# A graph layer's kernel: row decoding by two matmuls, an absolute value and a saturating addition, with 48 groups picked whole

## The chip, the cores and the metric

The kernel runs on one core of one Trainium2 chip. The metric is device microseconds of one execution, the median over several runs. Engines are named as in the profile: PE (TensorE matmuls), PEld (its weight loads), DVE (VectorE), ACT (ScalarE), POOL (GpSimd) and SP (SyncE, which issues most DMAs).

## The reference, cut to what matters

A graph layer over 6250 nodes of 64 features and 206250 edges, sorted by target node.

```python
h = jnp.maximum(_layernorm(x, axis=-1), 0.0)          # the table of node rows
msg = jax.nn.relu(h[src] + edge_attr)                 # one row per edge
agg = jax.ops.segment_sum(msg, dst, num_segments=6250)
z = h + agg
x = x + (jax.nn.relu(z @ W1 + b1) @ W2 + b2)
```

All of it is float32. The costly parts are `h[src]`, a gather of 206250 rows of 256 bytes from a table that the kernel itself makes, and the segment sum.

## The kernel before, in words

**Groups, sets, units.** Edges come in groups of 768 (128 partitions, 6 columns each), 269 groups in all. The first five are handled in the head. The others are bound into sets (`GROUPS`, line 63): a set is two groups, or one. Each set has six columns of 128 edges whose rows are *picked* by PE. In a set of two groups these are the last three columns of each group, and the other three columns of each (six in all) are *gathered* by POOL with one indirect DMA per column (`gather`, line 236). In a set of one group all six columns are picked and POOL gathers nothing for it; such a group is listed in `WHOLE`. Before the change there are 150 sets, 36 of them of one group. The loop (`both_units`, line 942) runs one unit per set; units alternate between even and odd ones, which have their work written out in two different orders. The order on each engine is the order in which the code stands, nothing is rescheduled.

**Picking.** The table stands in SBUF as two float16 parts per value (`hp`: 64 columns of high parts, 64 of low parts). DVE compares (`find` line 594, tile `found`; `back` line 606, tile `backs`) make one-hot matrices in float16; PE multiplies with them (`across_of` line 624, tile `half`), ACT copies the result to SBUF (`across`), PE transposes (`turn`), ACT copies again (`picked`), PE picks (`pick`, line 652). ACT copies the picked rows to the float16 tile `both` (`decode_parts`, line 716).

**Decoding.** The high part carries, as its sign, one more bit for the last place of the value. `decode_minus` (line 722) lets DVE make `minus`, the negated negative part of `both`. `decode_sum` (line 727) adds up, for each of six 128-column pieces, three matmuls of 64 columns in the PSUM bank `joint`: `both` with `join` (high times 2048 plus low), `minus` with `weigh_sign` (which turns the sign of the high part round), `minus` with `weigh_last` (the last place). `decode_add` (line 739) adds the result, scaled, from `joint` to the edge rows `ea` on DVE; `xg_add` (line 747) adds the gathered rows on DVE; `messages` (line 753) is one relu over the set's `ea` on ACT, a unit after the addition; `window_sum` (line 769) sums the messages on PE by one-hot matmuls of float32. The decoded sums and the window sums share the bank `joint`, in different columns. `sums` run only in even units, for two sets at a time.

**Queues.** SP issues the loads of `sources` and `spots` (768 KB each, once in two units), of the edge rows (`attr_set`, line 258) and the stores. POOL issues the gathers. Those of the first `AHEAD` = 6 sets are issued before the loop; the others stand in `pending` (line 269), and `passes` (line 273) issues one of them each time that the PE work written so far, added up from planned nanoseconds, has grown by `SPREAD` (1110 ns in the first 18 units, 1190 ns behind). A gather so issued carries a dependency on the PE instruction at which it was issued, so it cannot start before that instruction is done. The rows go into a ring of `RING` = 10 tiles `xg`. `ranked` and `counted_by_columns` prepare, once in three units, where each edge's row is to be found (`rank_of` and its neighbours).

Of the kernel before, what the change touches and what calls it, by code (L numbers as in the profile page):

```python
# [9 lines left out]

F32 = mybir.dt.float32
# [9 lines left out]
P = 128  # L21
G = 6
# [19 lines left out]
H = 3  # L42
# [16 lines left out]
HEAD, PAIR = 2 * RG - 1, 4 * RG - 3  # L59
SINGLES, DOUBLES = 3, 11  # L60
assert F0 + SINGLES * HEAD + DOUBLES * PAIR == NG + 1 and SETS == 3
# [16 lines left out]
PLACED = [0, 2, 6, 22, 38, NCH]  # L78
RING, AHEAD, EAS = 10, 6, 4
SPREAD = 1110, 1190  # L80
# [8 lines left out]
def kernel(  # L89
# [25 lines left out]
    FIRST = (F0 + HEAD) * G  # L115
# [61 lines left out]
    weigh_sign = const.tile([P, D], F16, name="weigh_sign")  # L177
    weigh_last = const.tile([P, D], F16, name="weigh_last")
    nc.vector.scalar_tensor_tensor(join, ident[:, :D], FINE, ident[:, D:], op0=ALU.mult, op1=ALU.add)
    for t, by in ((weigh_sign, 2 * FINE), (weigh_last, -FINE * HALF_LAST)):  # L180
        nc.vector.tensor_scalar_mul(t, ident[:, :D], by)
# [122 lines left out]
    def stretches(t_sb, c0, c1):  # L304

        wide = c0 >= 2 * SINGLES
        n, size, chunks = ((c1 - c0) // 4, PAIR, 4) if wide else ((c1 - c0) // 2, HEAD, 2)
# [173 lines left out]
    def ln_rows(r, n, v):  # L481
        h = x_rows(r, n)
        nc.vector.reciprocal(v, v)
        nc.vector.tensor_scalar_mul(v, v, UP)
# [18 lines left out]
    def ln_turned():  # L503
        zv = z[:D, :NP].rearrange("d (p r) -> d p r", r=RR)
        for pt, r, n in turned_rows:
            nc.scalar.activation(zv[:, :, r:r + n], pt[:, :n].rearrange("d u p -> d p u"), AF.Copy, scale=1.0 / UP)
        turned_rows.clear()

    def ln_parts(r, m, h):
# [3 lines left out]
        nc.scalar.copy(hi, h)  # L513
        nc.scalar.mul(rest, h, FINE)
# [9 lines left out]
        nc.vector.tensor_tensor(hi, hi, sign, ALU.mult)  # L524

    def add_attr(y, xg, ea):
        nc.vector.scalar_tensor_tensor(y, xg, 1.0 / UP, ea, op0=ALU.mult, op1=ALU.add)

    def combine(xg, ea, n):
        add_attr(xg[:, :n], xg[:, :n], ea[:, :n])  # L530
        nc.scalar.activation(ea[:, :n], xg[:, :n], AF.Relu)
        return ea
# [171 lines left out]
    def first_messages(g):  # L704
        ea, xg = ring(eas, g), rows_of(g)
        if g < RAW:
            yield from norm_edges(xg)
            nc.vector.tensor_tensor(ea, ea, xg, ALU.add)
        else:
            add_attr(ea, xg, ea)  # L710
        nc.scalar.activation(ea, ea, AF.Relu)
        msgs[g] = ea
# [25 lines left out]
    def decode_add(k):  # L738
        n = len(GROUPS[k])
        ea = eas[(k + RAWS) % EAS][:, :n]  # L740
        to = ea[:, :, G - H:] if n == 2 else ea[:, 0].rearrange("p (i j) d -> p i j d", i=2)
        to = to.rearrange("p i j d -> p i (j d)")
        nc.vector.scalar_tensor_tensor(to, joint[:, :2 * H * D].rearrange("p (i s) -> p i s", i=2),  # L743
                                       1.0 / (UP * FINE), to, op0=ALU.mult, op1=ALU.add)

    def xg_add(k):
        if len(GROUPS[k]) == 2:
            ea, xg = eas[(k + RAWS) % EAS], xgs[(k + RAWS) % RING]
            to = ea[:, :, :G - H].rearrange("p g j d -> p g (j d)")
            nc.vector.scalar_tensor_tensor(to, xg.rearrange("p g j d -> p g (j d)"), 1.0 / UP, to, op0=ALU.mult, op1=ALU.add)  # L750
# [180 lines left out]
    def joint_out(k):  # L931
        decode_add(k)
# [7 lines left out]
    def both_units(k):  # L940
# [7 lines left out]
        if odd:  # L948
# [20 lines left out]
            if k > 1:  # L969
                messages(k - 2)  # L970
# [11 lines left out]
            next(decoding, None)  # L982
            weave(compared, counted, others)
# [8 lines left out]
        else:  # L992
# [5 lines left out]
            if k > 1:  # L998
                messages(k - 2)
# [32 lines left out]
            next(decoding, None)  # L1032
# [279 lines left out]
```

## Time and profile before

| | before |
|---|---|
| median of three runs | 992.82 us (987.42 to 995.36) |
| the profiled execution | 989.2 us, its span 987.4 us |
| busy, share of the span: PE | 905.7 us, 92% |
| DVE | 922.7 us, 93% |
| ACT | 780.2 us, 79% |
| POOL | 749.1 us, 76% |
| mean granted PE clock | 0.968 |

The span runs from the first to the last instruction of the program on the core; 1.8 us of the profiled execution lie outside it. Busy time counts an instant once however many instructions of an engine overlap in it. [...] For ACT and DVE the profile's duration of an instruction also overlaps a little with its successor.

### The profile page before, as it was taken

What the parts mean: (1) busy time and instruction counts of PE and PEld (TensorE: products, weight loads), DVE (VectorE), ACT (ScalarE), POOL (GpSimd) and SP (SyncE); (2) the same over time, 40 slices, a digit from 0 to 9 for tenths busy, and PEclk for the clock granted to TensorE, in tenths of its full rate; (3) what the DMA queues carried; (4) which work ended last, traced back from release to release, by engine and by line L of the source; (5) the groups of instructions that cost most, each with busy time, mean ns of one, the idle gap of its engine ahead of it and who ended that gap; (6) DMA issues with size and microseconds to landing.
All of it is one profiled execution on the core that took longest, in us unless ns stands there. A gap on an engine that the chain in (4) does not pass through costs nothing.

```text
span 987.4 us, 35954 instructions
## 1 busy us (share of the span) xinstructions
PE 905.7 (92%) x13996; PEld 728.2 (74%) x13996; DVE 922.7 (93%) x2314; ACT 780.2 (79%) x1623; POOL 749.1 (76%) x727
## 2 busy tenths in 40 slices
PE   2249999999999989999999999999999999999986
PEld 1137777878877778787887777887877787787874
DVE  8898999989999999999999899999999999999975
ACT  6528888878888878888888788887887888888873
POOL 7877777777777777777777777777777777777771
PEclk9559999999999999999999999999999999999998
DMA  7436667666766666776766766766766666676841
GB/s 222 140 100 196 192 230 232 208 226 210 217 218 210 216 216 205 223 240 217 225 215 205 227 215 212 261 202 202 243 214 212 223 217 228 214 234 208 272 146 36
DMA packets 93833, 205.63 MB, mean 208 GB/s; under 512 B 24537, under 2 KB 62042, under 8 KB 93658
## 3 DMA queue, kind: packets, MB, share of 16 engines
q1 hardware_dynamic: 70762, 179.87, 51.1%
q0 software_dynamic: 22784, 23.38, 12.8%
q8 instruction: 112, 1.84, 0.7%
q14 instruction: 63, 0.52, 0.2%
q10 hardware_dynamic: 112, 0.03, 0.0%
HBM read 199.07 MB, written 4.13 MB: 206 GB/s over the span
## 4 chain that ended last, share of the span: by engine, by line
PE 60%; DVE 19%; DMA 12%; issue 3%; ACT 3%; DVEq 1%; POOL 1%; SPq 0%; ACTq 0%; POOLq 0%
PE pick L655 19%; PE half L633 13%; DMA xg<-h_rows,src_sb 9%; PE joint L769 8%; PE turn L644 7%; DVE backs L611 6%; PE joint L734 6%; DMA sources<-source_row 2%; PE rows L432 2%; DVE ea L743 2%; DVE found L601 2%; ACT ea L755 2%; PE rows L366 1%; PE half L628 1%; PE rows L808 1%
## 5 line engine op out<-in xcount | busy, mean ns | idle before, releaser
L241 POOL DMA_INDIRECT xg<-h_rows,src_sb x682 | 711.5, 1043 | 207.9 <-issue 52.7
L655 PE MATMUL pick<-backs,picked 128*128 128x384 f16 x1800 | 437.4, 328 | 0.0
L650 ACT COPY picked<-turn 128x512 f16<-128x512 f16 x450 | 262.6, 584 | 69.2 <-PE turn L644 62.0
L639 ACT CAST across<-half 128x512 f16<-128x512 f32 x450 | 264.9, 589 | 18.6 <-PE half L633 10.5
L633 PE MATMUL half<-found,hp 128*128 128x128 f16 x3600 | 276.5, 220 | 0.0
L611 DVE TENSOR_SCALAR backs<-spots,ids 128x1536 f16<-128x1536 int16 x450 | 275.4, 647 | 0.0
L633 PEld LDWEIGHTS <-hp 128*128 128x128 f16 x3600 | 234.5, 98 | 37.9 <-issue 0.6
L601 DVE TENSOR_SCALAR found<-sources,nodes_of 128x1536 f16<-128x1536 int16 x300 | 191.8, 672 | 1.1 <-issue 0.8
L655 PEld LDWEIGHTS <-picked 128*128 128x128 f16 x1800 | 157.3, 99 | 34.0 <-issue 0.3
L644 PE MATMUL turn<-ident_h,across 128*128 128x128 f16 x1800 | 175.8, 220 | 1.7 <-ACT picked L650 1.7
L755 ACT ACTIVATE ea<-ea 128x768 f32<-128x768 f32 x150 | 115.6, 770 | 55.0 <-DVE ea L743 50.5
L644 PEld LDWEIGHTS <-across 128*128 128x128 f16 x1800 | 123.0, 98 | 38.8 <-issue 6.0
L720 ACT CAST both<-pick 128x384 f16<-128x384 f32 x300 | 146.0, 487 | 3.2 <-PE pick L655 3.2
L769 PEld LDWEIGHTS joint<-oh,ea 128*64 128x64 f32 x3176 | 101.2, 138 | 48.9 <-DVE ea L743 24.6
L769 PE MATMUL joint<-oh,ea 128*64 128x32 f32 x3176 | 112.5, 224 | 20.3 <-DVE ea L743 11.6
L734 PE MATMUL joint<-join,both 128*128 128x64 f16 x900 | 127.0, 194 | 0.0
L734 PE MATMUL joint<-weigh_sign,minus 128*128 128x64 f16 x900 | 126.5, 194 | 0.6 <-DVE minus L724 0.5
L734 PE MATMUL joint<-weigh_last,minus 128*128 128x64 f16 x900 | 126.4, 194 | 0.0
L734 PEld LDWEIGHTS <-minus 128*128 128x128 f16 x1800 | 96.9, 98 | 16.5 <-DVE minus L724 1.3
L743 DVE SCALAR_TENSOR_TENSOR ea<-joint,ea 128x384 f32<-128x384 f32 x150 | 82.0, 547 | 22.5 <-PE joint L734 21.7
L734 PEld LDWEIGHTS <-both 128*128 128x128 f16 x900 | 88.1, 99 | 1.7
L696 DVE TENSOR_TENSOR oh<-slot,slots 128x384 f32<-128x384 int16 (+1 forms) x151 | 76.1, 504 | 0.1
(131 smaller groups left out, 777.0 us busy)
## 6 DMA issues: line engine op xcount, KB each, us to landing
sources<-source_row SPq DMA_DIRECT2D x75, 768.0 KB
spots<-spot_rows SPq DMA_DIRECT2D x75, 768.0 KB
ea<-in_edge_attr_dram SPq DMA_DIRECT2D x112, 384.0 KB
xg<-h_rows,src_sb POOLq DMA_INDIRECT x682
ea<-in_edge_attr_dram SPq DMA_DIRECT2D x44, 192.0 KB
xb<-in_x_dram SPq DMA_DIRECT2D x12, 128.0 KB
out_dram<-o SPq DMA_DIRECT2D x12, 128.0 KB
h_rows<-x SPq DMA_DIRECT2D x3, 384.0 KB
```

What stands on the lines that cost most here:

```text
L241: it = nc.gpsimd.indirect_dma_start(out=xg[:, j, :], out_offset=None, in_=rows[:, :], in_offset=bass.IndirectOffsetOnAxis(ap=idx[:, j:j + ...
L601: nc.vector.tensor_scalar(found[d][:, b * PARTS + m:b * PARTS + m + PARTS // 2].rearrange("p m u s -> p (m u s)"), sources[d][:, m * 4 * S ...
L611: nc.vector.tensor_scalar(backs[2 * d + u // 2][:, q].rearrange("p u v e -> p (u v e)"), spots[d].bitcast(I16)[:, u * VERSIONS * H * P:(u ...
L633: last = nc.tensor.matmul(ps[:, j * P:(j + 1) * P], hp[:, b * PARTS + m].rearrange("p t d -> p (t d)"), found[d][:, b * PARTS + m].rearran ...
L639: nc.scalar.copy(across[d, q].rearrange("p u j s -> p j u s"), ps.rearrange("p (j u s) -> p j u s", j=J, u=4))
L644: passes(nc.tensor.transpose(ps[:, u * P:(u + 1) * P], ac[:, u].rearrange("p j s -> p (j s)"), ident_h), 56)
L650: nc.scalar.copy(picked[d][:, q].rearrange("p u d -> p (u d)"), turned.pop((d, q)))
L655: it = nc.tensor.matmul(pick_banks[(2 * k + i) % 3][:, :H * P], picked[d][:, q, u], backs[k][:, q // VERSIONS, i, q % VERSIONS, :], start= ...
L720: nc.scalar.copy(fetched[k][:, i], pick_banks[(2 * k + i) % 3][:, :H * P])
L734: it = nc.tensor.matmul(to, rows[:, i, j * P:(j + 1) * P], weights, start=(n == 0), stop=(n == len(terms) - 1))
L755: nc.scalar.activation(msg, msg, AF.Relu)
L769: last = nc.tensor.matmul(pa[i * D:(i + 1) * D], msg[:, j, :], oh[:, j, :], start=(j < lo + 2), stop=(j >= G - 2))
```

## The change

The sign of the picked high part is no longer turned round by a matmul: both parts of the table now carry the sign (`ln_parts` multiplies high and low part by it), so the joined sum comes out negated or not, `weigh_last` takes the sign that fits, and an absolute value on ACT (`decode_out`) makes the row and scales it, out of PSUM into a new float32 tile `exact` of two buffers. `minus` is made by ACT. The additions on DVE become a custom instruction, `TENSOR_ADD_SAT`, which adds two tensors and limits the sum, here from below by 0: addition and relu in one. So `messages` is no longer an ACT instruction, and its place in the units falls away. The table of rows is no longer scaled by 4096 in memory. And the sets are cut otherwise: 156 sets, of which 48 have one group; four sets' gathers instead of six stand ahead of the loop. In the built programs 646 gathers of `h_rows` into `xg` stand in place of 682; 30 of the 682 stood ahead of the loop, and 18 of the 646 do.

```diff
-HEAD, PAIR = 2 * RG - 1, 4 * RG - 3
-SINGLES, DOUBLES = 3, 11
+ONE, TWO = 2 * RG - 1, 2 * RG - 2
+SINGLES, DOUBLES = 4, 22
...
-for h in range(SINGLES + 2 * DOUBLES):
-    last = h >= SINGLES and (h - SINGLES) % 2
+for h in range(SINGLES + DOUBLES):
     GROUPS += [(g, g + 1), (g + 2,), (g + 3, g + 4)]
     g += 5
-    GROUPS += [(g, g + 1), (g + 2,), (g + 3, g + 4)] if last else [(g, g + 1), (g + 2, g + 3), (g + 4, g + 5)]
-    g += 5 if last else 6
+    GROUPS += [(g, g + 1), (g + 2,), (g + 3, g + 4)] if h >= SINGLES else [(g, g + 1), (g + 2, g + 3), (g + 4, g + 5)]
+    g += 5 if h >= SINGLES else 6
...
-RING, AHEAD, EAS = 10, 6, 4
-SPREAD = 1110, 1190
+RING, AHEAD, EAS = 10, 4, 4
+SPREAD = 1112, 1267
...
-        nc.vector.tensor_tensor(hi, hi, sign, ALU.mult)
-
-    def add_attr(y, xg, ea):
-        nc.vector.scalar_tensor_tensor(y, xg, 1.0 / UP, ea, op0=ALU.mult, op1=ALU.add)
+        both = hp[:, r:r + m]
+        nc.vector.tensor_tensor(both, both, sign.unsqueeze(2).to_broadcast([PP, m, 2, D]), ALU.mult)
+
+    def add_relu(ea, xg):
+        nc.vector._custom_dve(TENSOR_ADD_SAT, out=ea, in0=xg, in1=ea, s0=float("inf"), s1=0.0)
...
-        nc.vector.tensor_scalar(minus, fetched[k], -1.0, 0.0, op0=ALU.mult, op1=ALU.max)
+        nc.scalar.activation(minus, fetched[k], AF.Relu, scale=-1.0)
...
-                terms = (both, join), (minus, weigh_sign), (minus, weigh_last)
+                terms = (both, join), (minus, weigh_last)
...
-    def decode_add(k):
-        n = len(GROUPS[k])
-        ea = eas[(k + RAWS) % EAS][:, :n]
-        to = ea[:, :, G - H:] if n == 2 else ea[:, 0].rearrange("p (i j) d -> p i j d", i=2)
-        to = to.rearrange("p i j d -> p i (j d)")
-        nc.vector.scalar_tensor_tensor(to, joint[:, :2 * H * D].rearrange("p (i s) -> p i s", i=2),
-                                       1.0 / (UP * FINE), to, op0=ALU.mult, op1=ALU.add)
+    exact = {}
+
+    def decode_out(k):
+        exact[k] = work.tile([P, 2, H * D], F32, name="exact", bufs=2)
+        nc.scalar.activation(exact[k].rearrange("p i s -> p (i s)"), joint[:, :2 * H * D], AF.Abs, scale=1.0 / (UP * FINE))
...
-        nc.scalar.activation(msg, msg, AF.Relu)
+        to = msg[:, :, G - H:] if len(gs) == 2 else msg[:, 0].rearrange("p (i j) d -> p i j d", i=2)
+        add_relu(to.rearrange("p i j d -> p i (j d)"), exact.pop(k))
...
     def joint_out(k):
-        decode_add(k)
+        messages(k)
...
-            if k > 1:
-                messages(k - 2)
...
             next(decoding, None)
             next(decoding, None)
+            decode_out(k - 1)
             weave(compared, counted, others)
```

On ACT, in one unit in the middle of the loop before the change, the relu of an earlier set (`ea`) stands among the copies:

```order
L650 COPY picked<-turn 128x512
L639 CAST across<-half_194 128x4x4x32
L720 CAST both<-pick_198 128x384
L755 ACTIVATE ea_150<-ea_150 128x768
L650 COPY picked<-turn 128x512
L639 CAST across<-half_195 128x4x4x32
L720 CAST both<-pick_199 128x384
L650 COPY picked<-turn 128x512
L639 CAST across<-half_194 128x4x4x32
```

In the changed kernel a unit at a like place reads so; `exact` is the absolute value out of PSUM, and `minus` the negated part:

```order
L735 ACTIVATE exact<-joint 128x384
L636 CAST across<-half_192 128x4x4x32
L713 CAST both<-pick_195 128x384
L717 ACTIVATE minus<-both 128x768
L647 COPY picked<-turn 128x512
L636 CAST across<-half_193 128x4x4x32
L713 CAST both<-pick_196 128x384
L647 COPY picked<-turn 128x512
L636 CAST across<-half_192 128x4x4x32
L647 COPY picked<-turn 128x512
L735 ACTIVATE exact<-joint 128x384
```

So ACT has two instructions per set, one of 768 and one of 384 elements, where it had one of 768 (384 in a set of one group).

On DVE, the end of an even unit and the start of the odd one behind it, before:

```order
L743 SCALAR_TENSOR_TENSOR ea_147<-joint,ea_147 128x2x192
L687 ISA
L687 TENSOR_TENSOR z<-z,joint 128x32
...
L696 TENSOR_TENSOR oh<-slot,slots 128x384
L750 SCALAR_TENSOR_TENSOR ea_148<-xg_152,ea_148 128x2x192
L724 TENSOR_SCALAR minus<-both 128x768
L611 TENSOR_SCALAR backs<-spots,ids 128x1536 x3
```

And in the changed kernel, where the rows named ISA at L525 are the custom instruction:

```order
L525 ISA ea_145<-exact,ea_145 128x2x192
L684 ISA
L684 TENSOR_TENSOR z<-z,joint 128x32
...
L693 TENSOR_TENSOR oh<-slot,slots 128x384
L608 TENSOR_SCALAR backs<-spots,ids 128x1536
```

`minus` has left DVE, and the addition at the end of a unit reads `exact`, which ACT writes, in place of `joint`, which PE writes.

## Rows read from the trace of the kernel before

**Rows 1.** Busy time by stretch: PE, PEld, DVE, ACT, POOL, clock, DMA; the loop
```profile
100.00:950.00 850.00, 832.39 (x13096) 672.33 (x13094) 814.21 (x2023) 703.96 (x1482) 657.85 (x631) 1.00 0.68 220
```

**Rows 2.** One line's instructions: the picks, 12 per set; min/median/max ns, first to last
```profile
L655 PE MATMUL pick<-backs,picked x1800: 323/326/524, 79.7 to 973.1; 128*128 128x384 f16 x180
```

**Rows 3.** Groups of instructions on DVE: busy us, mean ns; idle before
```profile
L611 DVE TENSOR_SCALAR backs<-spots,ids 128x1536 f16<-128x1536 int16 x450 | 275.4, 647 | 0.0
L601 DVE TENSOR_SCALAR found<-sources,nodes_of 128x1536 f16<-128x1536 int16 x300 | 191.8, 672 | 1.1 <-issue 0.8
L743 DVE SCALAR_TENSOR_TENSOR ea<-joint,ea 128x384 f32<-128x384 f32 x150 | 82.0, 547 | 22.5 <-PE joint L734 21.7 <-PE turn L644 0.7
L750 DVE SCALAR_TENSOR_TENSOR ea<-xg,ea 128x384 f32<-128x384 f32 x114 | 62.7, 550 | 0.5 <-issue 0.5
L724 DVE TENSOR_SCALAR minus<-both 128x768 f16<-128x768 f16 x150 | 54.1, 361 | 2.9 <-ACT both L720 2.9
L375 DVE TENSOR_REDUCE rank_of<-rows 128x18 f16<-128x432 f32 x50 | 29.9, 597 | 0.8 <-PE rows L366 0.8
...
L379 DVE SCALAR_TENSOR_TENSOR spot<-part,rank_of 128x18 int16<-128x18 f16 x50 | 9.0, 179 | 0.1
...
L524 DVE TENSOR_TENSOR hp<-hp,sign 128x768 f16<-128x768 f16 x3 | 1.7, 552 | 1.3 <-ACT sign L522 1.3
```

**Rows 4.** Timeline of DVE: start us, duration us; the negated part and its successor
```profile
562.91 0.35 DVE L724 TENSOR_SCALAR minus<-both 128x768 f16<-128x768 f16 x1
563.18 0.59 DVE L375 TENSOR_REDUCE rank_of<-rows 128x18 f16<-128x432 f32 x1
```

**Rows 5.** Who waited for whom: us in total, times, longest us
```profile
ACT ea L755 <- DVE ea L743: 50.5, 52, 3.2
PEld joint L769 <- DVE ea L743: 24.6, 35, 2.6
DVE ea L743 <- PE joint L734: 21.7, 27, 5.3
DVE found L596 <- DMA sources<-source_row: 13.2, 18, 3.1
PEld joint L769 <- ACT ea L755: 9.8, 19, 1.8
```

**Rows 6.** Groups of instructions on ACT
```profile
L720 ACT CAST both<-pick 128x384 f16<-128x384 f32 x300 | 146.0, 487 | 3.2 <-PE pick L655 3.2
L755 ACT ACTIVATE ea<-ea 128x768 f32<-128x768 f32 x114 | 96.5, 847 | 52.0 <-DVE ea L743 48.0 <-DVE backs L611 3.8
L755 ACT ACTIVATE ea<-ea 128x384 f32<-128x384 f32 x36 | 19.0, 528 | 3.0 <-DVE ea L743 2.5 <-issue 0.2
L522 ACT ACTIVATE sign<-sign 128x768 f16<-128x768 f16 x3 | 2.4, 828 | 0.0
```

**Rows 7.** Timeline of ACT: a relu of 768 elements and the copy behind it
```profile
609.37 0.84 ACT L755 ACTIVATE ea<-ea 128x768 f32<-128x768 f32 x1 [1.38 <-DVE ea L743]
610.12 0.57 ACT L650 COPY picked<-turn 128x512 f16<-128x512 f16 x1
```

**Rows 8.** Group of the gathers on POOL
```profile
L241 POOL DMA_INDIRECT xg<-h_rows,src_sb x682 | 711.5, 1043 | 207.9 <-issue 52.7 <-PE pick L655 36.0 <-PE half L633 27.4
```

**Rows 9.** Busy time by stretch, tile `xg` alone: additions on DVE, gathers on POOL
```profile
87.00:966.00 879.00, 61.02 (x111) 680.51 (x652) 0.99 0.68 218
```

**Rows 10.** The chain that ended last: start us, us, what
```profile
552.54 0.17 PE joint L734 x6
552.71 0.22 PE turn L644 x4
...
553.11 0.33 PE pick L655 x2
553.43 0.45 PE half L633 x8
...
554.38 5.43 DMA xg<-h_rows,src_sb
```

More of the change, by code (lines that the diff above doesn't have):

```diff
@@ L9 @@
 from concourse._compat import with_exitstack
+from concourse.dve_ops import TENSOR_ADD_SAT
 F32 = mybir.dt.float32
@@ L58 @@
 RG = 2 * SETS
-HEAD, PAIR = 2 * RG - 1, 4 * RG - 3
-SINGLES, DOUBLES = 3, 11
-assert F0 + SINGLES * HEAD + DOUBLES * PAIR == NG + 1 and SETS == 3
+ONE, TWO = 2 * RG - 1, 2 * RG - 2
+SINGLES, DOUBLES = 4, 22
+assert F0 + SINGLES * ONE + DOUBLES * TWO == NG + 1 and SETS == 3
 GROUPS = []
 g = F0
-for h in range(SINGLES + 2 * DOUBLES):
-    last = h >= SINGLES and (h - SINGLES) % 2
+for h in range(SINGLES + DOUBLES):
     GROUPS += [(g, g + 1), (g + 2,), (g + 3, g + 4)]
     g += 5
-    GROUPS += [(g, g + 1), (g + 2,), (g + 3, g + 4)] if last else [(g, g + 1), (g + 2, g + 3), (g + 4, g + 5)]
-    g += 5 if last else 6
+    GROUPS += [(g, g + 1), (g + 2,), (g + 3, g + 4)] if h >= SINGLES else [(g, g + 1), (g + 2, g + 3), (g + 4, g + 5)]
+    g += 5 if h >= SINGLES else 6
 KS = len(GROUPS)
@@ L77 @@
 QW = Q // VERSIONS
-PLACED = [0, 2, 6, 22, 38, NCH]
-RING, AHEAD, EAS = 10, 6, 4
-SPREAD = 1110, 1190
+PLACED = [0, 2, 8, 24, 40, NCH]
+RING, AHEAD, EAS = 10, 4, 4
+SPREAD = 1112, 1267
 UP, FINE = 2.0 ** 12, 2.0 ** 11
@@ L114 @@
     dst_sb = const.tile([P, CP], I32, name="dst_sb")
-    FIRST = (F0 + HEAD) * G
+    FIRST = (F0 + ONE) * G
     nc.sync.dma_start(out=src_sb[:, :FIRST], in_=src_main[:, :FIRST])
@@ L176 @@
     join = const.tile([P, D], F16, name="join")
-    weigh_sign = const.tile([P, D], F16, name="weigh_sign")
     weigh_last = const.tile([P, D], F16, name="weigh_last")
     nc.vector.scalar_tensor_tensor(join, ident[:, :D], FINE, ident[:, D:], op0=ALU.mult, op1=ALU.add)
-    for t, by in ((weigh_sign, 2 * FINE), (weigh_last, -FINE * HALF_LAST)):
-        nc.vector.tensor_scalar_mul(t, ident[:, :D], by)
+    nc.vector.tensor_scalar_mul(weigh_last, ident[:, :D], FINE * HALF_LAST)
     upper = const.tile([P, P], F16, name="upper")
@@ L306, in stretches @@
         wide = c0 >= 2 * SINGLES
-        n, size, chunks = ((c1 - c0) // 4, PAIR, 4) if wide else ((c1 - c0) // 2, HEAD, 2)
+        n, size, chunks = (c1 - c0) // 2, TWO if wide else ONE, 2
         assert n * chunks == c1 - c0 and (wide or c1 <= 2 * SINGLES)
@@ L505, in ln_turned @@
         for pt, r, n in turned_rows:
-            nc.scalar.activation(zv[:, :, r:r + n], pt[:, :n].rearrange("d u p -> d p u"), AF.Copy, scale=1.0 / UP)
+            nc.scalar.copy(zv[:, :, r:r + n], pt[:, :n].rearrange("d u p -> d p u"))
         turned_rows.clear()
@@ L512, in ln_parts @@
         sign = lnp.tile([PP, m, D], F16, name="sign")
-        nc.scalar.copy(hi, h)
-        nc.scalar.mul(rest, h, FINE)
+        nc.scalar.mul(hi, h, UP)
+        nc.scalar.mul(rest, h, UP * FINE)
         yield
@@ L707, in first_messages @@
             yield from norm_edges(xg)
[L708 to L712, printed above, removed]
+        msgs[g] = combine(xg, ea, G)
         yield
@@ L748, in xg_add @@
             ea, xg = eas[(k + RAWS) % EAS], xgs[(k + RAWS) % RING]
-            to = ea[:, :, :G - H].rearrange("p g j d -> p g (j d)")
-            nc.vector.scalar_tensor_tensor(to, xg.rearrange("p g j d -> p g (j d)"), 1.0 / UP, to, op0=ALU.mult, op1=ALU.add)
+            add_relu(ea[:, :, :G - H].rearrange("p g j d -> p g (j d)"), xg.rearrange("p g j d -> p g (j d)"))
     def messages(k):
@@ L997, in both_units @@
                 decode_minus(k - 1)
-            if k > 1:
-                messages(k - 2)
             next(picking, None)
@@ L1032, in both_units @@
             next(decoding, None)
+            if k:
+                decode_out(k - 1)
             next(picking, None)
@@ L1208 @@
     decode_minus(KS - 1)
-    messages(KS - 2)
     for k in (KS - 2, KS - 1):
@@ L1213 @@
     weave(joined(KS - 1))
+    decode_out(KS - 1)
     xg_add(KS - 1)
     weave(joint_out(KS - 1))
-    messages(KS - 1)
     weave(sums(KS - 1))
```

4 lines of the change are left out of this document (1 added, 3 removed).

## The prediction

> **What bounds the kernel now.** I read the page's busy shares first, then the loop alone by stretches. Between 100 and 950 us DVE is busy 814.2 of 850 us, 95.8%, ACT 82.8%, POOL 77%, PE 97.9% [rows 1]. PE's share is no load: a pick lasts 326 ns [rows 2], but in the chain two follow each other in 0.33 us, eight half matmuls take 0.45, four turns 0.22, six decode matmuls 0.17 [rows 10]. The picks, 12 per set, run from 79.7 to 973.1 us [rows 2]: 893 us for 150 sets, T = 5.96 us per set. Of this DVE works 0.958 x 5.96 = 5.71 us and ACT 4.94.
>
> The waits say who bounds whom. DVE's own waits are few: 21.7 us for PE's decode sums in 27 sets and 13.2 us for the `sources` load [rows 5]. PE and ACT wait for DVE: ACT's relu 50.5 us, PE's window sums 24.6 us, and 9.8 us more for that relu [rows 5]. So DVE sets the pace, with a chain DVE addition, ACT relu, PE window sums, PE decode, DVE addition that closes on it.
>
> The engine that its share hides is POOL. From 87 to 966 us it does 652 gathers [rows 9], 1.348 us each. Its idle time is 207.9 us over 682 gathers, 0.30 each [rows 8]: the same short gap before every one, no long wait at all. So POOL is working back to back through the whole loop, behind the pace that the code plans for it, and its last gathers come within ten microseconds of the last pick. DVE's additions of gathered rows nevertheless idle only 0.5 us [rows 3], so the gathers are in time, by the lead of six sets. POOL is a second limit just under the first: 682 gathers fit this span and hardly a shorter one.
>
> **The change part by part.** The sum is made against the profiled execution, 989.2 us, which lies 3.6 us under the median of 992.8; I carry the difference over to the median.
>
> *DVE loses `minus`.* 150 of them, 361 ns each [rows 3], but the next instruction starts 0.27 us behind its start while it still lasts 0.35 [rows 4]: instructions overlap by some 0.08 us. What goes is 150 x 0.27 = 40.5 us (54.1 if the overlap is not counted).
>
> *The additions keep their number per set and their size.* The custom instruction is not in the trace. It handles 384 float32 elements and two inputs, as the instructions that it replaces do; those took 547 ns reading PSUM and 550 ns reading SBUF [rows 3]. Below, the cheapest 768-element row is 361 ns, so 0.19 us per instruction less, times 264 (156 and 108 of them) = -50 us; above, if it ran like two instructions, 264 x 0.55 = +145 us. I take the nearest rows, which have its shape and input count: no change.
> [...]
>
> *Six more sets.* Per set DVE has three `backs`, two `found`, one addition: (275.4 + 191.8 + 82.0) / 150 = 3.66 us, and the ranking groups, seven of them from L375 to L379, 141 us in all, 0.94 per set [rows 3]. Less 0.08 us of overlap on some eight instructions this is about 4.0 us per set, 24 us for six. Six fewer additions of gathered rows give back 6 x 0.47 = 2.8 us.
>
> DVE in the loop: -40.5 + 24 - 2.8 = -19 us. With its waits at the same 4.2% of the time this is -20 us of loop.
>
> *PE comes out even.* Per set 18 decode matmuls of 0.028 us become 12; 2700 of them become 1872, -23 us. Six more sets bring 12 picks (0.165), 24 halves (0.056), 12 turns (0.055) and 12 decode matmuls each [rows 10]: 4.3 us, +26 us. So PE has no gain of its own, and none is counted; its room is in the waits of [rows 5].
>
> *ACT gets more.* In: `minus`, 768 elements of float16, like the 828 ns row; `exact`, 384 elements out of PSUM, like `both`, 487 ns. Out: the relu, 847 ns in 114 sets, 528 in 36 [rows 6]. Start to start a 768-element instruction takes 0.75 us where its row says 0.84 [rows 7], so 0.74 + 0.40 - 0.67 = +0.47 us per set. ACT's work rises from 4.94 to 5.41 us per set, 844 us for 156 sets, against DVE's 5.71 x 150 - 19 = 837. ACT, which had 17% of the loop to spare, is then as full as DVE. That is the cover that the move uses up. What it costs I bound from both sides. Below nothing: the addition no longer needs a relu behind it before the window sums, and the waits for the relu, 9.8 us on PE [rows 5], go. Above: in the sets in which DVE already waits for the decode, 27 of 150, the absolute value now stands between, 0.49 us plus a copy in front of it in ACT's queue of 0.47: 26 us. I take +4, near the lower end: between decode and window sums two engines have to act before and after, only in the other order, and most sets (123 of 150) do not wait for the decode.
>
> *Gathers.* There are 36 fewer, 49 us of POOL's time. In the first 24 sets, though, five of six sets still have six gathers, 8.1 us of POOL every 1.2 sets. With four sets ahead, POOL runs out of head gathers 12 x 1.35 = 16 us earlier, before the loop starts at 79.7, and stands still, as a pending gather waits for a PE instruction of the loop. Sets 4 to 23 then need 17 x 6 = 102 gathers: the last starts at 81 + 101 x 1.348 = 217 us and lands up to 5.4 us after its start [rows 10], at about 222.5. At 5.62 us per set DVE wants it at 79.7 + 24 x 5.62 + 2 = 217. Some 6 us are lost there, in the additions of gathered rows that wait for nothing today. Behind set 24 only four of six sets gather, 24 x 1.348 = 32.4 us in 6 x 5.62 = 33.7: POOL keeps up and the loss is not repeated. Range of this term: 0 if POOL does a gather in 1.25, which is 0.945 busy (its quickest) and the gap of 0.30, to 12 if it needs 1.40.
>
> *Head and tail.* Four sign multiplications cover twice the elements: one row is 552 ns [rows 3], so up to +2.2 us; four small scalings go. At the end the absolute value stands where the relu stood. I take +1.
>
> Sum: -20 + 4 + 6 + 1 = -9 to -10 us with DVE's price; with the DVE overlap uncounted (54.1) it would be -23, with the upper ends of ACT and gathers +18. From 989.2 this gives 979 to 980, from the median 992.8 about 983. I put it at **982**. A measurement tells about 1%, 10 us, from no change; the forecast lies at that edge.
>
> **The rivals.**
>
> *The gathers eat the gain.* If POOL's 1.348 us does not get better, the first 24 sets run at the old pace whatever DVE does, and the later ones at 33.7 us per six sets have only 1.3 us to make good. Place: the first additions of gathered rows, up to about 230 us. For it: POOL's gap of 0.30 before every gather [rows 8]. Against: it is over by set 26, and POOL has 49 us less to do in all. Time: 12 to 15 us lost, 988 to 991.
>
> *ACT becomes the bound (slower).* Place: the addition at the end of each unit, which now waits for ACT's absolute value, and the copies `across` and `picked`, which PE needs at once as there is one `turn` bank. ACT at 844 us fills a loop of 875 to 96%; no engine of the trace that hands work to and fro has done that except DVE at 95.8%. If ACT reaches only 92%, the loop is 917 us against 893: +24 us, 1017 us. It is slower than before from the point where ACT's fill stays under 94.5% (844 / 893). For it: the copies are short and in order, each waits for a PE result, 0.5 us at a time. Against: the largest wait that ACT has today for another engine but PE, 50.5 us for the additions [rows 5], goes with the relu.
>
> *PE's and DVE's waits go as well.* With the relu out of the chain the 24.6 and 9.8 us that PE waits at the window sums and the 21.7 us that DVE waits for the decode shrink [rows 5]. Half of them gone is worth 25 to 28 us of PE or DVE time, of which perhaps half shows: 965 to 972.
>
> *The custom instruction is not what it says.* At the price of two instructions it costs 145 us on DVE, 1110 us or more.
>
> **How the numbers follow.** Forecast (970 to 986): 0.43. Gathers eat the gain: 0.22. ACT bound: 0.20. Waits go as well: 0.12. Custom instruction slow: 0.03. Faster by over 1% (under 983): about three quarters of the forecast and all of the waits case, and a little of the gathers case, 0.46. Slower by over 1% (over 1003): most of the ACT case and the custom case, 0.20. Within 1%: 0.34. The range takes the waits case from 962 and the ACT case up to 1005, where its fill is about 93.5%; a custom instruction cheaper by its lower bound would reach under it, one at its upper bound far over it, and both are left out.
>
> **What would show it.** Right: the custom instruction near 550 ns; DVE busy about 895 us; ACT busy over 860; a group of waits at the additions of gathered rows before 235 us and none after; POOL's idle gap longer than 0.30 behind set 30. Wrong: the additions of `exact` waiting for ACT in more than 60 sets, or DVE under 92% of the loop with PE and ACT waiting for each other (ACT bound); gathers waited for in the middle of the loop; a custom instruction of another length; DVE's waits falling well under 36 us, or a loop under 860 us.

## The result, and the profile after

The change makes the kernel slower by about 1%. The changed kernel takes 1001.88 us (median of 5, 999.62 to 1007.79), the kernel before in the same series 992.49 us (986.59 to 995.36): ratio 1.012, 95% interval 1.0094 to 1.0145. Repeated later (below) the medians were 1002.39 and 991.05 us, the ratio 1.0078 (1.0056 to 1.0099). The forecast of 982 us lies on the wrong side of no change; the measured time lies inside the range given, near its upper end.

The profiled execution is the slowest of its five, 1007.8 us (span 1006.0), 6 us over the median; that of before lay 3.6 us under its own. So the medians give the size of the difference, and the two profiles show where it is.

| | before | after |
|---|---|---|
| DVE busy | 922.7 us, 93% | 897.6 us, 89% |
| ACT busy | 780.2 us, 79% | 861.7 us, 86% |
| PE busy | 905.7 us, 92% | 920.3 us, 91% |
| POOL busy | 749.1 us, 76% | 721.3 us, 72% |

The loop of the changed kernel by busy time, columns as in [rows 1]:

```profile
100.00:950.00 850.00, 827.37 (x12345) 656.94 (x12343) 773.25 (x1907) 765.85 (x1655) 628.01 (x596) 0.99 0.68 219
```

The picks of the changed kernel, as in [rows 2]:

```profile
L652 PE MATMUL pick<-backs,picked x1872: 322/326/567, 79.8 to 991.3; 128*128 128x384 f16 x188
```

T, the time per set from the first to the last pick, is 911.5 / 156 = 5.84 us, where it was 5.96. A set is 0.11 us quicker, and there are six more. DVE's fill of the loop fell from 95.8% to 773.25 / 850 = 91.0%. Its work fell much as forecast; the loop did not follow it.

Groups of instructions of the changed kernel, as in [rows 3], [rows 6] and [rows 8]:

```profile
L239 POOL DMA_INDIRECT xg<-h_rows,src_sb x646 | 682.5, 1057 | 248.3 <-PE half L630 54.4 <-issue 53.0 <-PE pick L652 40.0
L608 DVE TENSOR_SCALAR backs<-spots,ids 128x1536 f16<-128x1536 int16 x468 | 290.5, 656 | 0.3 <-PE pick L652 0.3
L717 ACT ACTIVATE minus<-both 128x768 f16<-128x768 f16 x156 | 134.1, 860 | 2.5
L735 ACT ACTIVATE exact<-joint 128x384 f32<-128x384 f32 x156 | 77.5, 497 | 2.6 <-PE joint L727 2.6
L525 DVE CUSTOM_DVE_ANT_1 ea<-exact,ea 128x384 f32<-128x384 f32 x108 | 59.7, 553 | 37.2 <-ACT exact L735 37.1
L525 DVE CUSTOM_DVE_ANT_1 ea<-xg,ea 128x384 f32<-128x384 f32 x108 | 59.5, 551 | 6.3 <-DMA xg<-h_rows,src_sb 3.1 <-DMA source_row<-source 2.7 <-issue 0.5
L525 DVE CUSTOM_DVE_ANT_0 ea<-exact,ea 128x384 f32<-128x384 f32 x48 | 26.6, 554 | 22.0 <-ACT exact L735 20.4 <-ACT picked L647 1.3
```

The custom addition costs what the additions before it cost, 551 to 554 ns against 547 and 550. ACT's two instructions cost 860 and 497 ns, as taken. POOL is no longer back to back: its idle time per gather is 248.3 / 646 = 0.38 us, where it was 0.30. The 6.3 us in front of the additions of gathered rows are almost all in two places, both before 235 us, as DVE's timeline of the changed kernel shows:

```profile
222.69 0.56 DVE L525 CUSTOM_DVE_ANT_1 ea<-xg,ea 128x384 f32<-128x384 f32 x1 [3.06 <-DMA xg<-h_rows,src_sb]
231.26 0.56 DVE L525 CUSTOM_DVE_ANT_1 ea<-xg,ea 128x384 f32<-128x384 f32 x1 [2.72 <-DMA source_row<-source]
```

Who waited for whom in the changed kernel, as in [rows 5]:

```profile
DVE ea L525 <- ACT exact L735: 57.5, 47, 6.2
ACT picked L647 <- PE turn L641: 53.3, 97, 3.5
PEld joint L760 <- DVE oh L693: 15.6, 20, 1.7
```

In [rows 5] ACT and PE waited for DVE. ACT's largest wait before the change, which those rows leave out, was one for PE, and it was longer than now:

```profile
ACT picked L650 <- PE turn L644: 62.0, 164, 1.8
```

Now DVE itself has the largest wait, for ACT, and ACT waits for PE as before. The chain that ended last shows whose work stands behind both, in the middle of the loop (start us, us, what):

```profile
611.73 0.22 PE turn L641 x4
611.96 0.45 PE half L630 x8
612.40 0.49 PE pick L652 x3
612.89 1.17 PE joint L760 x36
...
615.92 0.59 ACT picked L647
616.51 0.32 ACT exact L735
616.83 0.32 issue
617.15 0.62 ACT across L636
617.76 0.74 ACT minus L717
618.50 0.48 ACT picked L647
619.03 0.38 PE turn L641 x4
...
624.45 1.52 PE joint L760 x48
```

From 598 to 616 us the chain is PE's matmuls one after another, then one stretch of 3 us on ACT (`picked`, `exact`, `across`, `minus`, `picked`), then PE again. PE is at its rate here, and that rate had not been added up before: the last row gives 0.032 us for one matmul of the window sums, and the chain before the change gives the same:

```profile
597.82 1.52 PE joint L769 x48
```

The loop has 3176 of them, 0.68 us per set before the change. With the 18 decode matmuls, 12 picks, 24 halves and 12 turns of [rows 10], 4.5 us, and about 0.6 us of matmuls for ranking, the layer and the half products of 512 columns (an estimate from their pieces of the chain), PE had some 5.8 us of work in a T of 5.96, as much as DVE's 5.71; after, some 5.6 in 5.84. The chain before the change bears this out: from 574.8 to 601.9 us it is PE's matmuls without a break, and four sets in it (48 picks, 575.66 to 599.34 us) take 5.9 us each. Over the whole span PE had 60% of that chain and DVE 19%.

### The profile page after: what moved, and what is told of

The parts are those of the page before. It is cut to its first block, busy times and chain, and to the rows that moved or that the text cites. A ratio compares the mean times of both kernels' runs of the same rounds, so it can differ in the third digit from the quotient of the medians.

```text
span 1006.0 us, 34733 instructions
## 1 busy us (share of the span) xinstructions
PE 920.3 (91%) x13479; PEld 727.1 (72%) x13479; DVE 897.6 (89%) x2224; ACT 861.7 (86%) x1836; POOL 721.3 (72%) x691
## 4 chain that ended last, share of the span: by engine, by line
PE 54%; DVE 13%; ACT 11%; DMA 8%; POOL 6%; issue 6%; DVEq 1%; SPq 0%; POOLq 0%; ACTq 0%
PE pick L652 16%; PE half L630 12%; PE joint L760 8%; PE turn L641 8%; DVE backs L608 5%; DMA xg<-h_rows,src_sb 5%; ACT picked L647 4%; PE joint L727 4%; POOL xr L239 3%; DMA sources<-source_row 3%; ACT across L636 3%; ACT minus L717 2%; POOL xg L239 2%; DVE ea L525 2%; PE rows L430 2%
## 5 line engine op out<-in xcount | busy, mean ns | idle before, releaser
L239 POOL DMA_INDIRECT xg<-h_rows,src_sb x646 | 682.5, 1057 | 248.3 <-PE half L630 54.4
L652 PE MATMUL pick<-backs,picked 128*128 128x384 f16 x1872 | 452.3, 329 | 2.8 <-DVE backs L608 2.8
L647 ACT COPY picked<-turn 128x512 f16<-128x512 f16 x468 | 279.6, 597 | 59.4 <-PE turn L641 53.3
L636 ACT CAST across<-half 128x512 f16<-128x512 f32 x468 | 281.7, 602 | 11.1 <-PE half L630 7.1
L608 DVE TENSOR_SCALAR backs<-spots,ids 128x1536 f16<-128x1536 int16 x468 | 290.5, 656 | 0.3 <-PE pick L652 0.3
L630 PE MATMUL half<-found,hp 128*128 128x128 f16 x3744 | 287.2, 220 | 0.0
L717 ACT ACTIVATE minus<-both 128x768 f16<-128x768 f16 x156 | 134.1, 860 | 2.5
L525 DVE CUSTOM_DVE_ANT_1 ea<-exact,ea 128x384 f32<-128x384 f32 x108 | 59.7, 553 | 37.2 <-ACT exact L735 37.1
L727 PEld LDWEIGHTS <-minus 128*128 128x128 f16 x936 | 73.2, 98 | 17.1 <-issue 2.1
L735 ACT ACTIVATE exact<-joint 128x384 f32<-128x384 f32 x156 | 77.5, 497 | 2.6 <-PE joint L727 2.6
```

The source lines that it names most:

```text
L239: it = nc.gpsimd.indirect_dma_start(out=xg[:, j, :], out_offset=None, in_=rows[:, :], in_offset=bass.IndirectOffsetOnAxis(ap=idx[:, j:j + ...
L608: nc.vector.tensor_scalar(backs[2 * d + u // 2][:, q].rearrange("p u v e -> p (u v e)"), spots[d].bitcast(I16)[:, u * VERSIONS * H * P:(u ...
L630: last = nc.tensor.matmul(ps[:, j * P:(j + 1) * P], hp[:, b * PARTS + m].rearrange("p t d -> p (t d)"), found[d][:, b * PARTS + m].rearran ...
L636: nc.scalar.copy(across[d, q].rearrange("p u j s -> p j u s"), ps.rearrange("p (j u s) -> p j u s", j=J, u=4))
L647: nc.scalar.copy(picked[d][:, q].rearrange("p u d -> p (u d)"), turned.pop((d, q)))
L652: it = nc.tensor.matmul(pick_banks[(2 * k + i) % 3][:, :H * P], picked[d][:, q, u], backs[k][:, q // VERSIONS, i, q % VERSIONS, :], start= ...
```

## The experiments

The first question was which part of the change costs: the decoding, the cut into 156 sets, or the shorter lead of the gathers. The second was which engine a set's 5.84 us belong to. Each kernel is the changed one but for the edit shown, unless said otherwise. The lines under an edit quote what was expected.

**The decoding alone.** Cut, `PLACED` and `AHEAD` as before the change.

```diff
-SPREAD = 1112, 1267
+SPREAD = 1080, 1155
```

> The new decoding with the old cut: 150 sets, 36 of one group, 682 gathers, six sets' gathers ahead, the gathers' spacing shortened by 3% to fit the shorter plan. PE theory (the loop is bound by PE's own work, which the change leaves at 857 to 860 us, so that six more sets took what six fewer matmuls per set gave): PE has 25 us less to do than before, POOL's 682 gathers at 1.348 us still need 919 us, so 975 to 988 us. ACT theory (ACT with two instructions in place of one is what slows the loop): not faster than before, 992 or more, as ACT has the same work per set as in the changed kernel.

Measured: 980.26 us, 990.51 before; ratio 0.990 (0.988 to 0.992). The decoding is a gain of 10 us. Its picks, its gathers and the group of its additions of gathered rows:

```profile
L653 PE MATMUL pick<-backs,picked x1800: 322/326/527, 78.5 to 959.8; 128*128 128x384 f16 x180
```

```profile
L240 POOL DMA_INDIRECT xg<-h_rows,src_sb x682: 940/947/2645, 47.0 to 955.9; - x171
```

```profile
L240 POOL DMA_INDIRECT xg<-h_rows,src_sb x682 | 702.4, 1030 | 207.9 <-issue 56.1 <-PE pick L653 35.7 <-PE half L631 31.1
L526 DVE CUSTOM_DVE_ANT_1 ea<-xg,ea 128x384 f32<-128x384 f32 x114 | 62.8, 551 | 11.8 <-DMA xg<-h_rows,src_sb 7.9 <-issue 3.9
```

T is 5.875 us. POOL has the gap of 207.9 / 682 = 0.30 us before every gather, runs until 4 us before the last pick, and DVE now waits for gathers. So with the old cut the decoding runs into POOL, the second limit that the prediction named.

**The cut alone.** The kernel before the change with the new cut, `PLACED` and `AHEAD`.

```diff
-SPREAD = 1110, 1190
+SPREAD = 1140, 1300
```

> The old decoding with the new cut: 156 sets, 48 of one group, four sets' gathers ahead, the spacing lengthened by 2.5% to fit the longer plan. PE theory: six sets more at 4.9 us of PE, +29 us, and 6 us of late gathers in the first 25 units: 1015 to 1030 us. ACT theory: ACT is as free as before, the 49 us less on POOL tell: 985 to 1000 us.

Measured: 1018.96 us; ratio 1.027 (1.025 to 1.030). Its picks:

```profile
L654 PE MATMUL pick<-backs,picked x1872: 326/326/567, 80.3 to 1008.5; 128*128 128x384 f16 x188
```

T is 928.2 / 156 = 5.95 us, that of before (5.96). But this profiled execution lies 6.8 us over its median, and that of before 3.6 us under its own. By the medians six more sets, with the shorter lead, cost 28 us, where six times T is 36: more sets of one group make a set shorter by a little, and not by enough.

**Six sets of gathers ahead.**

```diff
-RING, AHEAD, EAS = 10, 4, 4
+RING, AHEAD, EAS = 10, 6, 4
```

> The changed kernel with six sets' gathers ahead of the loop in place of four. Late gathers cost what the trace shows, 3.1 and 2.7 us at 222 and 231 us and what PE loses behind them: 993 to 997 us, and no addition of gathered rows waits. If they cost nothing in the end (PE bound throughout): 1000 to 1003.

Measured: 996.37 us; ratio 1.006 (1.004 to 1.008), 5.5 us under the changed kernel by the first series, 2 to 6 by the ratios. The waits for gathers are gone (6.3 us in the changed kernel):

```profile
L525 DVE CUSTOM_DVE_ANT_1 ea<-xg,ea 128x384 f32<-128x384 f32 x108 | 59.8, 553 | 0.5 <-issue 0.3 <-DMA xg<-h_rows,src_sb 0.2
```

So the term of 6 us for the shorter lead was about right. By these three runs the way from 990.5 to 1001.9 us is: decoding -10, cut with its spacing of the gathers +16 (from the first run to this one), lead +5.5 (2 to 6 by the ratios).

**`minus` back on DVE.**

```diff
-        nc.scalar.activation(minus, fetched[k], AF.Relu, scale=-1.0)
+        nc.vector.tensor_scalar(minus, fetched[k], -1.0, 0.0, op0=ALU.mult, op1=ALU.max)
```

> The changed kernel with the negated part made by DVE again, everything else as changed. ACT theory (the 768-element instruction in ACT's queue delays copies that PE waits for, and the absolute value that DVE waits for): 980 to 992 us. DVE theory (DVE's work per set sets the pace): 0.27 us more in each of 156 sets, 1015 us or more. PE theory alone: no change within 5 us.

Measured: 1014.59 us; ratio 1.024 (1.022 to 1.026). Its loop:

```profile
100.00:950.00 850.00, 816.17 (x12253) 652.97 (x12253) 805.36 (x2037) 663.59 (x1498) 633.00 (x590) 0.99 0.66 218
```

156 times 0.27 us, 42 us of DVE, cost 12 to 16 us, 0.3 to 0.4 for one, although ACT got 115 us back and fell to 78%. Moving `minus` was a gain, and ACT's fuller loop costs less than it brings.

**Taking work from ACT or PE, giving PE more, reordering ACT: first round.** In order: `minus` not made; a third matmul with weights of zeros; one matmul; the absolute value ahead of the copy before it.

```diff
-        minus = work.tile([P, 2, H * P], F16, name="minus", bufs=1)
-        nc.scalar.activation(minus, fetched[k], AF.Relu, scale=-1.0)
-        fetched[k] = fetched[k], minus
+        fetched[k] = fetched[k], fetched[k]
```

> The changed kernel without the instruction that makes `minus` (156 of 860 ns, 0.74 us from start to start): the matmul with `weigh_last` reads `both` in its place. The term for the last place of a value is then not the reference's; PE and DVE have the same work as in the changed kernel, ACT 0.74 us per set less. Theory 'PE paces, ACT only by hand-offs' (PE works 5.5 of 5.8 us per set): 0 to 10 us less than the changed kernel, 992 to 1002 us. Rival 'ACT is the bound': its work falls from 5.4 to 4.7 us per set, and the time by 20 us or more, to 980 us or under. Rival 'DVE is still the bound': no difference that can be measured.

```diff
-                terms = (both, join), (minus, weigh_last)
+                terms = (both, join), (minus, weigh_none), (minus, weigh_last)
...
-                    passes(it, 29)
+                    passes(it, 58 / 3)
```

> The changed kernel with a third matmul per piece, weights of zeros, so that the decoding again has 18 matmuls per set; the gathers are spaced as in the changed kernel. PE has 6 x 0.028 = 0.168 us per set more, 26 us in 156 sets; ACT and DVE have nothing more. Theory 'PE paces': 20 to 26 us more than the changed kernel, 1020 to 1028 us. Rivals 'ACT is the bound' or 'DVE is the bound': 0 to 5 us more. Theory 'three engines at 91 to 95% hand work to and fro': about half, 10 to 16 us more.

```diff
-                terms = (both, join), (minus, weigh_last)
+                terms = ((both, join),)
...
-                    passes(it, 29)
+                    passes(it, 58)
```

> The changed kernel with one decode matmul per piece in place of two: the last-place term is left out of the sum, `minus` is still made and read by nothing. The gathers are spaced as in the changed kernel. PE has 0.168 us per set less, 26 us in 156 sets; ACT and DVE the same. Theory 'PE paces': 15 to 25 us less than the changed kernel, 977 to 987 us. Rivals 'ACT is the bound' or 'DVE is the bound': 0 to 5 us less. Theory 'three engines hand work to and fro': about half of PE's part, 8 to 14 us less.

```diff
-            turn_at(3 * k + 8)
+            ps_at(3 * k + 8)
...
+            copy_at(3 * k + 8)
```

(`ps_at` is the PE half of `turn_at`, `copy_at` its ACT half, which now stands behind `decode_out`.)

> The changed kernel with the same instructions, PE's in the same order; on ACT the absolute value `exact` stands ahead of the copy `picked` that precedes it at a unit's end, instead of behind it. In the changed kernel `exact` starts 0.40 us after the last decode matmul, nearly always, and DVE's additions wait 57.5 us for it in 47 units. Theory 'hand-offs at the unit's end cost': the additions' wait falls by about 0.4 us in 47 units, 19 us, of which the late `picked` copy takes a part back: 5 to 12 us less than the changed kernel, 990 to 997 us. Rivals 'PE paces' or 'ACT is the bound': the late copy holds PE up as much as the early `exact` frees DVE: within 5 us, or more time where PE then waits for `picked`.

Measured: 1146.01, 1155.75, 1136.16 and 1144.75 us, with 1208.1 us for the kernel before: ratios 0.948 (0.941 to 0.954), 0.956 (0.952 to 0.961), 0.941 (0.936 to 0.945), 0.949 (0.941 to 0.956). These ran on a chip on which the kernel before takes 22% longer than in the first series. None of the expectations can be held against them, as the changed kernel was not run there, and only the step from one matmul to three, 19.6 us for 52 us of PE, can be read. The last section comes back to this chip. Three of the four were run again elsewhere; the reordering was run again only with the old cut.

**The changed kernel again.**

> The changed kernel once more, unchanged, beside the experiments that follow. The runs of the third matmul, the one matmul, the missing `minus` and the early absolute value fell on a chip on which the kernel before takes 1208 us instead of 990, so they can't be set against the changed kernel's 1002 us. On a chip where the kernel before takes about 990 us: 1002 us, ratio 1.009 to 1.015. On a chip where it takes about 1208 us: 1146 us, ratio 0.95, as the four runs there lie between 0.94 and 0.956 and the third and the single matmul lie symmetrically around it; theory 'PE is short of instructions there' expects the changed kernel, which has some 830 matmuls fewer than the kernel before, to gain there what it loses here.

Measured: the 1002.39 us of the first section, on a chip with 991.05 us for the kernel before. The next three ran with it.

**No `minus`, again.** The edit as above.

> The changed kernel without the instruction that makes `minus`; the matmul with `weigh_last` reads `both` in its place, so the term for the last place is not the reference's. PE and DVE have the same work as in the changed kernel, ACT 0.74 us per set less, 115 us in 156 sets. Beside the changed kernel of the same runs: theory 'PE paces, ACT only by hand-offs' 0 to 10 us less; rival 'ACT is the bound' 20 us less or more; rival 'DVE is the bound' no difference that can be measured.

Measured: 1001.85 us; ratio 1.009 (1.007 to 1.011). Nothing, for 115 us of ACT. Its loop, and the wait that took the work's place:

```profile
100.00:950.00 850.00, 825.82 (x12419) 661.57 (x12417) 781.40 (x1916) 672.39 (x1515) 627.63 (x598) 0.99 0.67 220
```

```profile
ACT picked L647 <- PE turn L641: 110.9, 129, 6.0
```

ACT's fill went from 90% to 79%, and it waits for PE 111 us instead of 53. ACT is not the bound.

**One matmul, again.** The edit as above.

> The changed kernel with one decode matmul per piece in place of two; the last-place term is left out of the sum, `minus` is still made and read by nothing. PE has 0.168 us per set less, 26 us in 156 sets; ACT and DVE have the same work. Beside the changed kernel of the same runs: theory 'PE paces' 15 to 25 us less; rivals 'ACT is the bound' or 'DVE is the bound' 0 to 5 us less; theory 'three engines hand work to and fro' 8 to 14 us less.

Measured: 994.19 us; ratio 1.002 (1.000 to 1.005): 5 us (by ratios) to 8 us (by medians) less than the changed kernel, for 26 us of PE. That is far from the 15 to 25 us of PE alone. By the medians it is the hand-off theory's figure, by the ratios it lies between that and the 0 to 5 us of the other two.

**The old cut with the absolute value first.** The first experiment with the reordering above.

> The new decoding with the old cut into 150 sets and six sets of gathers ahead (the first experiment, ratio 0.990 to the kernel before), and with the absolute value on ACT ahead of the copy `picked` that stood before it at a unit's end. Theory 'hand-offs at the unit's end cost': DVE's additions waited 47 us for the absolute value there in 43 units, and this falls by 0.4 us each: 5 to 12 us less than the first experiment, ratio 0.978 to 0.985. Rival 'POOL limits the late half there' (its gathers go back to back in the first experiment, the last one 11 us before the last pick): the first half gains 2 to 4 us, the second nothing: ratio 0.986 to 0.990. Rival 'PE paces': nothing, or a loss where PE then waits for `picked`.

Measured: 982.40 us; ratio 0.989 (0.986 to 0.993), the first experiment's. Who waited, and the group of the additions of gathered rows:

```profile
DVE ea L526 <- ACT exact L736: 39.1, 39, 7.0
```

```profile
L526 DVE CUSTOM_DVE_ANT_1 ea<-xg,ea 128x384 f32<-128x384 f32 x114 | 63.0, 552 | 21.9 <-DMA xg<-h_rows,src_sb 20.4 <-issue 1.5
```

The additions wait 8 us less for `exact` (47.1 in the first experiment) and 10 us more in front of the gathered rows (11.8 there). The wait moved to the gathers, which speaks for POOL as the limit of this cut; PE as the pace would have brought no gain either. (The first experiment's last gather starts 4 us before its last pick, not 11.)

**Less DVE.** The addition of gathered rows for one of three columns per group.

```diff
-            add_relu(ea[:, :, :G - H].rearrange("p g j d -> p g (j d)"), xg.rearrange("p g j d -> p g (j d)"))
+            add_relu(ea[:, :, 0], xg[:, :, 0])
```

> The changed kernel with the addition of gathered rows for one of their three columns per group only: 128 elements per partition in place of 384, 108 times; the other two columns' rows are not added. Gathers, PE and ACT have the same work; DVE about 0.35 us less in 108 of 156 sets, 38 us in all (estimate: 551 ns less a third of it). Beside the changed kernel's ratio of 1.008 to 1.011: theory 'DVE still paces': 25 to 38 us less, ratio 0.972 to 0.984. Theory 'PE paces': 0 to 5 us less, ratio 1.003 or more. Theory 'PE and DVE in turn, by hand-offs': 8 to 18 us less, ratio 0.990 to 1.001.

Measured: 990.19 us, 991.43 before; ratio 0.999 (0.997 to 1.001). The additions:

```profile
L525 DVE CUSTOM_DVE_ANT_1 ea<-xg,ea 128x128 f32<-128x128 f32 x108 | 30.9, 286 | 0.8 <-issue 0.7
```

DVE lost 28.6 us (108 times 551 less 286 ns), not 38, and the time 9 to 13 us. Not all of this is DVE's work: the additions no longer read two of the three columns and so no longer wait for their gathers, and the waits for late gathers, 6.3 us of idle time in the changed kernel, are gone with the work (0.8 us left). Beside the run with six sets ahead, which does not wait for gathers either, the gain is about 7 us (ratios 1.006 and 0.999), a quarter of the 28.6.

**Less DVE and less PE.** The two edits together.

> The run before, with one decode matmul per piece besides, so that DVE has 38 us and PE 26 us less than in the changed kernel (the last-place term and two of three gathered columns are left out of the sums). The one matmul alone gave about 8 us. Theory 'PE and DVE side by side, each nearly full': together more than the sum of the two alone, 25 us or more, ratio 0.984 or less. Theory 'a chain in which each gives its part': the sum of the two alone, 16 to 26 us, ratio 0.984 to 0.994. Theory 'POOL or a DMA queue holds from outside': no more than either alone.

Measured: 982.37 us; ratio 0.990 (0.987 to 0.993), 18 to 22 us under the changed kernel: about the sum of the two alone.

**Less of all three.** And without `minus`.

> The run before, with `minus` not made either: DVE 38, PE 26 and ACT 115 us less than in the changed kernel. Leaving out `minus` alone gave nothing. Theory 'ACT has room and only hands on': 0 to 8 us less than the run before. Theory 'ACT is the next bound behind the two': 20 us or more less than the run before.

Measured: 981.23 us; ratio 0.990 (0.987 to 0.993). Nothing more from ACT. The chain that ended last, late in the loop of this kernel:

```profile
710.28 1.27 DVE backs L608 x2
711.55 0.47 DVE ea L525
712.01 0.47 DVE oh L693
712.48 0.27 DVE found L593
```

With PE relieved the chain runs on DVE over this stretch, where the changed kernel's ran on PE. Over the whole span DVE's share of the chain is 36%, PE's 36%; in the changed kernel they are 13% and 54%.

**A third matmul, again.** The edit as above.

> The changed kernel with a third matmul per piece, weights of zeros: PE 26 us more, ACT and DVE nothing. Theory 'PE paces': 20 to 26 us more than the changed kernel, ratio 1.028 to 1.037. Theory 'PE and DVE in turn': 8 to 16 us more, ratio 1.016 to 1.027. Theory 'DVE still paces': 0 to 5 us more, ratio 1.008 to 1.016.

Measured: 1014.32 us; ratio 1.024 (1.021 to 1.028): 12 to 16 us more for 26 us of PE. From 600 to 612 us its chain is all PE, of which a piece:

```profile
604.66 0.16 PE pick L654
604.82 0.17 PE joint L729 x6
604.99 0.22 PE turn L643 x4
605.22 0.17 PE joint L729 x6
605.39 0.33 PE pick L654 x2
```

What follows from these: neither PE nor DVE is the bound alone. A microsecond taken from DVE is worth about 0.25 (7 of 28.6), one added to it 0.3 to 0.4 (12 to 16 of 42), one taken from PE 0.2 to 0.3, one added to PE about 0.5, and one from ACT nothing, while the other two are near full. The fastest kernel of the study is the new decoding with the old cut and the old lead, 1% faster than before and 2% faster than the changed kernel.

## Why the prediction was wrong

*DVE sets the pace: half right, and the step that failed.* The sum took DVE's work off the loop one for one ("DVE in the loop: -40.5 + 24 - 2.8 = -19 us. With its waits at the same 4.2% of the time this is -20 us of loop"). The instruction counts and durations in it hold. But DVE's idle share rose to 9%, because PE, with some 5.8 us of work in a T of 5.96, was as full as DVE. The term that failed is the -40.5 us for `minus`: put back on DVE, `minus` cost 12 to 16 us, and the whole new decoding brought 10 with the old cut. By the runs DVE's work shows in the time at 0.25 to 0.4. The prediction set PE's busy share aside as no load, priced the picks, halves, turns and decode matmuls, 4.5 us per set, and left out the window sums, 0.68 us, and the ranking and layer, some 0.6. From 4.5 us it looked as though PE had room; with all of them the load is 97% of T, and the busy share of 97.9% was near it. And where the waits were read as PE and ACT waiting for DVE, ACT's largest wait, 62.0 us for PE, was not among the rows.

*"PE comes out even. [...] its room is in the waits": the sum is sound, the room was not there.* The 23 us that the decoding takes from PE and the 26 us that six sets add show in the time as DVE's do. Per set DVE's and PE's savings together brought 5.96 to 5.78 us, the T of the run with six sets ahead (79.1 to 981.0 us, 156 sets), 0.18 us. The prediction expected (893 - 20) / 156 = 5.60, 0.36 us less. Over 156 sets that is 28 us, against a miss of 20 (1002 for 982). The +4 that the sum held for ACT, and the two profiles, which lie 2 us over and 4 us under their medians, are the rest.

*Six more sets, 24 less 2.8 us, and 6 for the lead: near.* With the old decoding cut and lead together cost 28 us, where these terms make 27. With the new one the cut alone cost 16 us, not 21; that it relieves POOL there is the likely reason, not a tested one. A set of one group takes a unit like any other: its picks, halves and turns on PE and its compares on DVE do not shrink, and only the addition of gathered rows goes.

*ACT's +4: small, as taken.* The additions wait for `exact` 57.5 us in 47 units, under the 60 sets that were to speak for ACT as the bound; DVE at 91% of the loop is under the 92% that were to speak for it too. The signs were mixed; the run without `minus` settles it, as 115 us less of ACT changed nothing. The rival "ACT becomes the bound" falls. It forecast the right sign for a reason that did not hold.

*Late gathers, 6 us: right*, in place (222 and 231 us), in size (6.3 us of waits, 2 to 6 us by the run with six ahead), and in not being repeated. The rival "the gathers eat the gain" is part of the truth: with the old cut the additions do wait for POOL's gathers. What the decoding alone would bring without that limit was not run.

*The custom instruction at the price of what it replaces: right*, 551 to 554 ns. The addition that now reads `exact` in SBUF takes 553 and 554 ns; the one that read `joint` in PSUM took 547.

*Waits go as well: no.* PE's largest wait at the window sums did fall, from 24.6 to 15.6 us, but PE's idle time in the loop grew from 17.6 to 22.6 us, and DVE's wait for the decoding, 21.7 us, became one of 57.5 for the absolute value behind it.

## What to carry to other kernels

Add up every engine's work per turn of the loop before naming the bound, PE's from the times of its matmuls in the chain and with all of them, the small float32 ones too: where two engines were near full (PE with an estimated 5.6 of 5.84 us per set, DVE at 91% of the loop), a microsecond taken from one was worth a quarter of itself here, and a move that adds turns to the loop adds work to both. A busy share that cannot be trusted as it stands, as PE's (a pick lasts 326 ns, two in the chain take 0.33 us), can still be near the load (97.9% of the loop beside a sum of 97%, before the change); the sum decides. A share that falls after a change while the time stays (DVE from 95.8% to 91%) says that the cover was another engine. And a change of several parts is worth measuring in parts: here the half that gains and the half that loses came together.

## What the runs showed of the hardware

One chip ran every kernel that was also run elsewhere far slower: 1208.1 us for the kernel before, which took 990.5 to 992.5 us in the four other series, and 1136.16 us for the kernel with one matmul, which took 994.19 elsewhere: 22% more for the one, 14% for the other. The durations of single instructions do not show it: in the run with the absolute value first, on that chip, and in the changed kernel picks take 326 and 326 ns at the median, custom additions of `exact` 556 and 553 ns, gathers 1043 and 1057 ns. One thing that differs is that PE sometimes stands still in the middle of a run of matmuls of one kind. PE's timeline of the run with the absolute value first, on that chip:

```profile
703.50 0.22 PE L630 MATMUL half<-found,hp 128*128 128x128 f16 x1
703.91 0.38 PE L630 MATMUL half<-found,hp 128*128 128x128 f16 x4 [0.19 <-issue]
704.65 0.33 PE L630 MATMUL half<-found,hp 128*128 128x128 f16 x3 [0.36 <-issue]
```

Eight half matmuls, otherwise 0.45 us in one piece, take 1.3 us with two stops that end by nothing that the profile shows. Such stops are rare: idle time that ends so in front of the half matmuls and their weight loads is 9.0 us over the span of this run (25 times), and 0.8 us (4 times) in the changed kernel on another chip. More time is lost in front of the transposes, where the weight loads wait for nothing that the profile shows: in the kernel with one matmul, on that chip and on the other,

```profile
PEld L641 <- issue: 108.4, 172, 1.8
```

```profile
PEld L641 <- issue: 27.3, 70, 0.8
```

The loop of the kernel with one matmul, there and on the other chip:

```profile
100.00:950.00 850.00, 746.42 (x10081) 572.05 (x10078) 683.44 (x1688) 680.98 (x1452) 550.92 (x525) 0.99 0.59 193
```

```profile
100.00:950.00 850.00, 814.50 (x11621) 640.25 (x11619) 789.82 (x1928) 772.99 (x1674) 628.25 (x604) 0.99 0.67 222
```

Each engine does 8 to 14% less in the same 850 us, at the same granted clock of 0.99. There the four kernels with the new decoding and the new cut were 4 to 6% faster than the kernel before; three of them were also run elsewhere, where they are 0.2 to 2.4% slower. Why PE stops and waits there, and why the kernel before suffers more, stays open: it was not traced on that chip.

A second figure that no run before this one had: the custom addition takes 286 ns for 128 elements and 551 for 384, so, as an estimate from these two, 1.04 ns per element and about 150 ns besides.
